# Two-layer sequence kernel: some small loads may be issued on ScalarE's queue, and the norm chains of the attention blocks get an earlier place in the order

## The chip, the cores and the metric

The kernel runs on one core of a Trainium2 chip. The metric is the device time of one execution in microseconds. The core's engines are TensorE (PE: matrix products, transposes; its weight loads are listed apart as PEld), VectorE (DVE), ScalarE (ACT), GpSimd (POOL) and SyncE (SP), which here does nothing but issue DMA transfers. Each engine works through its own instructions in order; semaphores order the engines among each other.

## The reference

The input x is 16 sequences of 256 tokens with 512 channels. Two layers follow each other. The first is a transformer layer with a self-attention, a cross-attention to a second sequence, and an MLP, each with a layer norm ahead of it and a residual sum behind it:

```python
ln_out = layernorm(hidden_states, ln1_s, ln1_b)
qkv = ln_out @ w_qkv + b_qkv
ctx = merge_heads(attention(split_heads(q), split_heads(k), split_heads(v), ltor_mask))
x = hidden_states + (ctx @ w_ao + b_ao)
ln_out = layernorm(x, ln2_s, ln2_b)
...                                   # q from x, k and v from encoder_states
x = x + cross_out
ln_out = layernorm(x, ln3_s, ln3_b)
return x + gelu(ln_out @ w1 + b1) @ w2 + b2
```

Attention has 16 heads of 32 channels and a mask: `scores * mask - 10000 * (1 - mask)`, then a softmax over 256 keys. The second layer mixes each token with the one before it, and carries a state of 16 x 16 for each of 32 heads along the 256 tokens:

```python
a = k_l[..., :, None] * v_l[..., None, :]
out = einsum('bhs,bhst->bht', r_l, faaaa * a + s)
s_new = a + w_l[..., None] * s
...
x = x + y * g @ Wo.T                  # y: out, normalized by head
xc = _ln(x, ln2_w, ln2_b)             # then the channel mix:
x = x + sigmoid(xr2 @ fWr.T) * (square(relu(xk2 @ fWk.T)) @ fWv.T)
```

## The kernel before, in words

**Stages.** The program works in phases, each over the 16 sequences, which it calls batches: A is the self-attention, B the cross-attention, C the MLP, D the token mixing and the projections r, k, v, w and g, I the part of the recurrence inside chunks of 8 tokens, and E the tail. C and D run twice, for batches 0 to 7 and 8 to 15; I is spread in small portions among C, D and E. Between phases the data lies in HBM: x1 after A, x2 after B, x3 after C, then s_r, s_k, s_v, s_w, s_g and what I makes of them (s_y, s_ks, s_rp, s_tot). By the profile A runs from 0 to some 690 us, B to some 1400, the halves of C and D to some 2700 and the tail to the end.

**Products.** Most fp32 products are made of three matmuls of a high and a low part (`mm3`, L495 to L514; the matmuls are L506, L507 and L508).

**Attention, A and B.** `attention` (L774) goes through the 64 groups of four heads. For a group: projection of q and k; scores (L723); on VectorE scale and mask (L730) and row extremes (L736); on ScalarE the exponential (L737); on VectorE a reciprocal of the sums (L740); on POOL the scaling (L743); on TensorE transposes of the probabilities (L756), their copy to SBUF on ScalarE or VectorE (`copy`, L487); and the product with V (L768). A batch ends with the store of x1 or x2.

**The norm chain.** `layer_norm` (L586 to L602) makes, for each half of 128 tokens, statistics (`lnst`, L593, VectorE) and their aggregate (`lnmv`, L594), then adds epsilon (L595, VectorE, the name `lnrs`), raises to the power -1/2 (L596, POOL, the same name), makes the offset (`lnnb`, L597, VectorE) and writes the normalized rows (`xh`), on VectorE or POOL (L600) or ScalarE (L601). TensorE transposes those rows at L613.

**The tail, E.** For each batch `states` (L1391) loads keys (KBc) and spreads them (L1346), and then, for each of two halves of the heads, loads Values with eight transfers of 32 KB into one of two VO tiles (L1410), makes products (L1419), copies the first column, scans (L1426, VectorE), copies (L1427, ScalarE or VectorE) and stores the states with four transfers (`sdr`). `starts` loads them again and spreads them (L1346). `reads` transposes (L1458) and copies (L1469), `heads` multiplies (L1487), and `output`, `residual`, `channels` and `finish` end the batch with products at L1536 and L1578. The functions of different batches are interleaved by the lists `LAG` and `TURNS`.

**What sets the order.** The program first collects all operations with what they read and write. `Sched.run` (L260) then goes through them with planned costs and gives out, step by step, the operation that can start earliest on any engine. An operation may have alternatives on several engines. The key by which one is picked is (L328)

```python
if len(o.alts) > 1:
    s += o.bias.get(e, 0.0)
kx = (max(s - o.urge, f), o.prio, a[1])
```

where `s` is the planned start on that engine, `f` the time at which the engine is free, `o.bias` a handicap for one of several engines, `o.urge` a lead in nanoseconds, and `o.prio` a rank (program order plus an entry of the table `PRIO`). `emit` (L427) looks up rank and urge under the phase and the name of what is written, such as `A.lnst`, and the bias under the phase: POOL has 400 ns in A and B. After an operation its engine's latency from the table `LAT` (L191; SP 950 ns, ACT 128) stands before the operations that wait for it. An operation of the kind `dma` (L479) has the engine SP alone, with 440 ns, and a planned transfer time `o.xfer`. The order so found is written out as each engine's order of instructions, and the chip keeps to it. So one changed number can move instructions in all phases.

Of the kernel before, what the change touches and what calls it, by code (L numbers as in the profile page):

```python
# [16 lines left out]
B, S, C = 16, 256, 512  # L17
# [168 lines left out]
class Sched:  # L186
# [73 lines left out]
    def run(self):  # L260
# [51 lines left out]
        while done < len(ops):  # L312
            best = None
            for e in engs:
                f, c = free[e], None
                for o, a in ready[e]:
                    s = o.t0[e] if o.t0[e] > f else f
                    if e in o.port and port > s:
                        s = port
                    if o.xfer and queues - self.AHEAD > s:  # L320
                        s = queues - self.AHEAD
                    for h in o.banks:
                        for e2, t in used.get(h, {}).items():
                            if e2 != e and t > s:
                                s = t
# [3 lines that stand above are left out]
                    if c is None or kx < c[0]:  # L329
                        c = (kx, o, a)  # L330
                if c is not None and (best is None or c[0] < best[0]):
                    best = c
            assert best is not None, "the streams block each other: " + str({k: [o.i for o in v][:3] for k, v in waits.items() if v})
            _, o, alt = best
            for a in o.alts:
                ready[a[0]].remove((o, a))
            k = can(o)
            if k is not None:
                waits.setdefault(k, []).append(o)
                continue  # L340
            o.eng, o.cost, fn = alt
            o.lat = self.LAT[o.eng]
            t0 = max(o.hold, o.t0[o.eng])
            woken = {}
            for h in sorted((h for h in o.tiles if h.cls is not None and h.t is None), key=lambda h: h.seq):
                if h.cls is not None and h.t is None:
                    t0 = max(t0, mem.ready(h))
                    mem.put(h)
                    woken[h.phase, h.tag, h.cls] = 1
            s = max(t0, free[o.eng])  # L350
            for h in o.banks:
                s = max([s] + [t for e2, t in used.get(h, {}).items() if e2 != o.eng])
            if o.eng in o.port:
                s = max(s, port)
                port = s + o.cost
            if o.xfer:
                s = max(s, queues - self.AHEAD)
            o.start, o.end = s, s + o.cost
            free[o.eng] = o.end
            for h in o.banks:  # L360
                used.setdefault(h, {})[o.eng] = o.end + o.lat
            if o.xfer:
                o.end = queues = max(o.end + self.START, queues) + o.xfer
            if not self.dry:
                fn()
                self.pin()
            for h in o.tiles:
                h.left -= 1
                if h.left == 0 and h.cls is not None:
                    mem.drop(h, o.end + o.lat)  # L370
                    woken[h.phase, h.tag, h.cls] = 1
                    woken[mem.SIZE[h.cls][0]] = 1
            done += 1
            for d in o.outs:
                p = ops[d]
                p.ndep -= 1
                if p.ndep == 0:
                    put(p)
            for k in woken:
                for p in waits.pop(k, []):  # L380
                    put(p)
# [5 lines left out]
def c_act(n, ptr=0, acc=0):  # L387
    return 76.0 + n / 1.2 + 85.0 * ptr + 125.0 * acc
# [14 lines left out]
def c_dma(nbytes, short=False):  # L403

    return nbytes / (146.0 if short else 290.0)


class Kern:
# [18 lines left out]
    def emit(self, eng, cost, fn, r=(), w=(), single=False):  # L427
# [5 lines left out]
        o.bias = BIAS.get(p, {})  # L433
        o.urge = URGE.get(p + "." + (h.split("_")[-1] if h[:1] == "k" and h[1:2].isdigit() else h), 0.0)
        return o
# [40 lines left out]
    def cols(self, ap, n, name):  # L476
        return self.konst([128, n], ap.rearrange("(k p) -> p k", p=128), name)

    def dma(self, h, out, in_, nbytes, r=(), w=None, short=False):  # L479
        o = self.emit("SP", 440.0, lambda: self.nc.sync.dma_start(out=out(), in_=in_()), r=r, w=[h] if w is None else w)  # L480
        o.xfer = c_dma(nbytes, short)
        return o

# [779 lines left out]
class Tail(Rec):  # L1263
# [127 lines left out]
    def states(self, b):  # L1391
# [6 lines left out]
        hk, hv = self.hin["ks"][0], self.hin["v2"][0]  # L1398
# [8 lines left out]
        for hf in range(2):  # L1407
            VO, Sc = self.VO[hf], tile("Sc", [128, 4, 8, 2, 16], "Sc")
            for n in range(8):
                self.dma(None, lambda n=n, VO=VO: VO[16 * n : 16 * n + 16, n, :, :].rearrange("p a v -> p (a v)"), lambda n=n, hf=hf: self.dap("v2", b * S * C + n * 16384 + 512 * hf, [[1024, 16], [1, 512]]), 32768, r=[(hv, b)], w=[(VO, n)])  # L1410
            for pg in (2 * hf, 2 * hf + 1):
                U = tile("p_u", [128, 16, 32], "pu")

                def mm(U=U, pg=pg, VO=VO, hf=hf):
                    for t in range(4):
                        for q in range(4):
                            p = 4 * pg + q
                            n = min(8, 31 - 8 * t)
                            nc.tensor.matmul(U[32 * q : 32 * q + 32, :, 8 * t + 1 : 8 * t + 1 + n].rearrange("p v n -> p n v"), lhsT=KB[t // 2][:, t % 2, p, :], rhs=VO[:, 0:n, 8 * t + p - 8 * hf, :], start=True, stop=True, tile_position=(0, 32 * q))  # L1419

                emit("PE", 900, mm, [VO] + KB, [(U, 1)])
                uc, d0 = (tile(n, [128, 16, 32], n) for n in ("uc", "d0"))
                self.copy(16, lambda U=U: U[:, :, 0], lambda pg=pg: s0[:, 4 * (b % 4) + pg, :], [s0], [(U, 0)])
                emit(("ACT", "POOL"), (c_act(512) + 43, 650), tuple(lambda d0=d0, pg=pg, f=f: f(out=d0(), in_=T[:, b % 4, pg, :].unsqueeze(1).to_broadcast([128, 16, 32])) for f in (nc.scalar.copy, nc.gpsimd.tensor_copy)), [T], [d0])
                flat = lambda t: t().rearrange("p v n -> p (v n)")
                emit("DVE", 1139, lambda uc=uc, d0=d0, U=U: nc.vector.tensor_tensor_scan(out=flat(uc), data0=flat(d0), data1=flat(U), initial=0.0, op0=ALU.mult, op1=ALU.add), [U, d0], [uc])  # L1426
                emit(("ACT", "DVE"), (1066, 700), tuple(lambda uc=uc, Sc=Sc, pg=pg, f=f: f(out=Sc[:, :, :, pg % 2, :].rearrange("p n r v -> p r n v"), in_=uc().rearrange("p v (r n) -> p r n v", n=4)) for f in (nc.scalar.copy, nc.vector.tensor_copy)), [uc], [(Sc, pg % 2)])  # L1427
            for q in range(4):
                self.dma(None, lambda q=q, hf=hf: dr[hf, :, :, q, :].rearrange("n c x -> c n x"), lambda q=q, Sc=Sc: Sc[32 * q : 32 * q + 32].rearrange("p n r g v -> p n (r g v)"), 131072, [Sc], [(dr, (q, hf))])
# [194 lines left out]
    "I": dict(rk=4, P=2, A=1, Y=1),  # L1624
}
PRIO = {"A.pq": -20, "B.pq": -20, "A.pv": 50, "B.x": -400, "B.pv": 50, "A.po": 20, "B.po": -100, "A.x": -50, "A.V": 50, "B.V": 50, "B.qkdr": 20, "B.pc": 20, "A.ks": -20, "A.xh": 20, "B.xh": 400, "B.ks": -20, "B.lnst": -400, "A.rin": -100, "B.rin": -100, "A.E": -50, "A.lnmv": 20, "B.lnmv": 20, "I.P3": -20, "C.xh": -400, "I.r": -100, "E.uc": 100, "D.tt": 20, "I.P2": 20, "C.h": -50, "I.k": 200, "D.s_v": -400, "D.th": -400, "C.ph": -50, "D.x3": -400, "I.v": -20, "I.Y": -100, "D.s_g": -200, "C.g": -200, "E.KBc": -50, "I.s_tot": 200, "C.lnst": 100, "C.po": 400, "D.s1": -400, "E.yT": -400, "E.SBc": -50, "E.xa": 100, "I.s_rp": 400, "E.wst": 20, "I.A": 50, "D.s_k": -20, "D.or": -20, "E.lnst": -20, "E.gr": -200, "C.xT": -200, "D.pt": 20, "D.pd": 50, "E.sq": -100, "C.x": -400, "C.lnmv": -20, "D.ov": 100, "D.x0": -20, "D.ok": 50, "D.lnmv": 100, "D.lnst": -50, "D.xx": -200, "E.gm": 20, "I.s_ks": -20, "D.x": -400, "D.x2": -100, "D.tdr": 100, "C.lnrs": 400, "E.xh": 50, "E.ptr": -100, "D.sx": 20, "E.pr": 200, "E.KB": -50, "D.ow": 100, "E.rp": 400, "D.pz": 50, "D.ptr": 20}
URGE = {n: 200 for n in ('E.gv', 'E.gr', 'E.gt', 'E.lnst', 'E.lnmv', 'E.lnrs', 'E.lnnb')}
AHEAD = [2, 2]
PARTS = [(0, 8), (8, 16)]
AFTER = [7, 4]  # L1630
# [110 lines left out]
```

## Time and profile before

| | |
|---|---|
| median of three runs | 3413.0 us (3410.54 to 3414.68) |
| profiled execution | 3407.0 us |
| span of the profiled execution | 3405.2 us |
| mean granted TensorE clock | 0.975 |
| instructions on TensorE, VectorE, ScalarE, POOL | 27210, 6701, 4750, 1932 |
| bytes moved, mean rate | 334.21 MB, 98 GB/s |
| loads of Values into VO tiles | 256, of 32 KB |

The span runs from the first to the last instruction of the profiled execution. Busy times are given by engine; matmuls are pipelined, and their ends are modelled. A row of the timeline has the start, the length, the engine, the line, the operation with what it writes and reads, and, in square brackets, the idle time of the engine just before it and what ended it. A row of the waits has a total, a number of times and the longest one. SPq is SP's queue of DMA issues. Lines of the form L480 are lines of the kernel before.

### The profile page before, as it was taken

The numbers are of one execution on the slowest core, as the hardware profiler recorded it, in microseconds if no ns is written. First come the engines' busy times: TensorE is split into PE (matmuls) and PEld (weight loads), VectorE is DVE, ScalarE is ACT, GpSimd is POOL, SyncE is SP. The second block draws the span as 40 slices with busy tenths as digits, with TensorE's granted clock in tenths as the row PEclk, the third lists the DMA queues.
The fourth block names the chain that finished last, engine by engine and source line by source line (L and its number), as shares of the span: only waits on it lengthen the run. The fifth ranks groups of instructions, "written<-read, shape, count | busy, mean of one in ns | idle before, by whom it ended". The sixth has DMA issues, their size and how long they took to land. (4 is left out here: it accounts for less than half of the span.)

```text
span 3405.2 us, 73366 instructions
## 1 busy us (share of the span) xinstructions
PE 3196.5 (94%) x27210; PEld 2627.1 (77%) x27210; DVE 2842.5 (83%) x6701; ACT 1878.1 (55%) x4750; POOL 1501.6 (44%) x1932
## 2 busy tenths in 40 slices
PE   7999999999999999899999999999799859999899
PEld 5788777777777777799998888999698745555577
DVE  7888888888888888876788889899889868888786
ACT  6666666666666666633334554434454547565654
POOL 3444444443444444300021127898112766767442
PEclk9999999999999999899999999999899969999999
DMA  3000000121111111310023554434345876765530
GB/s 101 26 26 32 27 29 28 35 79 44 45 45 45 45 45 54 104 33 13 32 75 125 170 180 131 124 117 121 106 152 160 251 230 189 211 195 177 172 120 32
DMA packets 321775, 334.21 MB, mean 98 GB/s; under 512 B 40294, under 2 KB 225166, under 8 KB 321418
## 3 DMA queue, kind: packets, MB, share of 16 engines
q1 hardware_dynamic: 321418, 329.52, 31.1%
q8 instruction: 216, 3.54, 0.4%
q14 instruction: 141, 1.16, 0.1%
HBM read 198.32 MB, written 131.10 MB: 97 GB/s over the span
## 5 line engine op out<-in xcount | busy, mean ns | idle before, releaser
L743 POOL TENSOR_SCALAR slot<-slot,k_rin 128x256 f32<-128x256 f32 x1024 | 489.2, 496 | 619.1 <-DVE k_rin L740 582.7
L492 POOL TENSOR_TENSOR slot<-slot,slot 128x512 f32<-128x512 f32 (+10 forms) x428 | 570.6, 1352 | 339.5 <-ACT slot L571 96.3
L737 ACT ACTIVATE slot<-slot,k_nmx 128x256 f32<-128x256 f32 x1024 | 507.8, 500 | 171.0 <-DVE k_nmx L736 148.5
L506 PE MATMUL bank<-slot,block 128*128 128x256 f32 x2048 | 584.8, 286 | 1.8 <-ACT slot L487 1.3
L507 PE MATMUL bank<-slot,block 128*128 128x256 f32 x2048 | 581.9, 284 | 2.1 <-DVE slot L578 1.4
L508 PE MATMUL bank<-slot,block 128*128 128x256 f32 x2048 | 580.9, 284 | 0.0
L506 PE MATMUL bank<-block,slot 128*128 128x512 f32 x1240 | 502.4, 405 | 4.4 <-DVE slot L577 2.9
L487 ACT ACTIVATE slot<-bank 128x512 f32<-128x512 f32 (+2 forms) x634 | 343.1, 571 | 291.0 <-PE bank L508 148.8
L508 PE MATMUL bank<-block,slot 128*128 128x512 f32 x1240 | 486.6, 392 | 4.5 <-DVE slot L578 2.7
L507 PE MATMUL bank<-block,slot 128*128 128x512 f32 x1240 | 486.4, 392 | 0.0
L506 PEld LDWEIGHTS bank<-slot,block 128*128 128x128 f32 x2048 | 393.5, 192 | 10.6 <-ACT slot L487 3.0
L507 PEld LDWEIGHTS bank<-slot,block 128*128 128x128 f32 x2048 | 393.6, 192 | 9.8 <-DVE slot L623 1.8
L736 DVE CUSTOM_DVE_ANT_0 slot<-slot,slot 128x256 f32<-128x256 f32 x1006 | 398.6, 443 | 0.0
L508 PEld LDWEIGHTS bank<-slot,block 128*128 128x128 f32 x2048 | 393.5, 192 | 0.0
L730 DVE SCALAR_TENSOR_TENSOR slot<-bank,slot 128x512 f32<-128x512 f32 x512 | 330.0, 680 | 53.4 <-PE bank L768 25.1
L756 PE MATMUL bank<-k_c,slot 128*128 128x128 f32 x2048 | 286.3, 280 | 17.6 <-POOL slot L743 13.4
L756 PEld LDWEIGHTS bank<-k_c,slot 128*128 128x128 f32 x2048 | 229.8, 142 | 88.5 <-POOL slot L743 57.5
L506 PE MATMUL bank<-slot,slot 128*128 128x256 f32 (+1 forms) x848 | 276.8, 326 | 13.9 <-ACT slot L577 11.5
L506 PEld LDWEIGHTS bank<-block,slot 128*128 128x128 f32 x1240 | 234.6, 189 | 65.4 <-issue 19.8
L507 PE MATMUL bank<-slot,slot 128*128 128x256 f32 (+1 forms) x848 | 275.5, 325 | 6.6 <-DVE slot L578 6.3
L508 PEld LDWEIGHTS bank<-block,slot 128*128 128x128 f32 x1240 | 233.8, 189 | 59.1 <-DVE slot L578 5.1
L508 PE MATMUL bank<-slot,slot 128*128 128x256 f32 (+1 forms) x848 | 275.0, 324 | 2.4 <-DVE slot L578 2.4
(203 smaller groups left out, 6467.7 us busy)
## 6 DMA issues: line engine op xcount, KB each, us to landing
slot<-in SPq DMA_DIRECT2D x153, 256.0 KB
slot<-x SPq DMA_DIRECT2D x64, 512.0 KB
x<-slot SPq DMA_DIRECT2D x48, 512.0 KB
slot<-in SPq DMA_DIRECT2D x32, 512.0 KB
sdr<-slot SPq DMA_DIRECT2D x128, 128.0 KB
slot<-sdr SPq DMA_DIRECT2D x32, 512.0 KB
s_k<-slot SPq DMA_DIRECT2D x16, 512.0 KB
s_w<-slot SPq DMA_DIRECT2D x16, 512.0 KB
```

Of the source, the lines that this page charges most:

```text
L487: self.emit(("ACT", "DVE"), (c_act(n), c_dve(n)), (lambda: nc.scalar.activation(out=out(), in_=in_(), func=AF.Copy), lambda: nc.vector.ten ...
L492: self.emit(("DVE", "POOL"), (c_dve(n), c_pool(n)), (lambda: nc.vector.tensor_tensor(out=out(), in0=in0(), in1=in1(), op=op), lambda: nc.g ...
L506: nc.tensor.matmul(o, lhsT=lh, rhs=rh, start=first and i == 0, stop=False)
L507: nc.tensor.matmul(o, lhsT=lh, rhs=rl, start=False, stop=False)
L508: nc.tensor.matmul(o, lhsT=ll, rhs=rh, start=False, stop=last and i == k - 1)
L730: emit("DVE", c_dve(512), lambda j=j, T=T: nc.vector.scalar_tensor_tensor(out=T(), in0=ps[j](), scalar=-scale, in1=mask(), op0=ALU.mult, o ...
L736: emit("DVE", c_dve(256) + 80, lambda T=T, j=j, qt=qt: nc.vector.tensor_tensor_reduce(out=T[:, qt, :], in0=T[:, qt, :], in1=negb[:, qt, :] ...
L737: emit("ACT", c_act(256, 1, 1), lambda T=T, Et=Et, j=j, qt=qt: nc.scalar.activation(out=Et[:, qt, :], in_=T[:, qt, :], func=AF.Exp, scale= ...
L743: emit("POOL", 470, lambda jj=jj, qt=qt: nc.gpsimd.tensor_scalar(out=E[jj][:, qt, :], in0=E[jj][:, qt, :], scalar1=rin[:, qt, jj : jj + 1] ...
L756: nc.tensor.transpose(pt[:, k, 128 * qt : 128 * qt + 128], E[j][:, qt, 128 * k : 128 * k + 128], self.ident())
```

## The change

The change has three parts. `dma` gets a parameter `two`: with it an operation has the alternatives SP (440 ns) and ACT (500 ns), ACT with a bias of 300 ns. It is set for Values' loads of the batches 0 to 4 of the tail, which are 80 of the 256; all other transfers stay on SP. The latency that is planned behind a transfer is that of SP, whichever engine issues it. And the table `URGE`, which had seven names of the tail with 200 ns, gets ten more with 200 ns: `lnst`, `lnmv`, `lnrs`, `lnnb` and `xh` of A and of B.

```diff
@@ Sched.run
-            o.lat = self.LAT[o.eng]
+            o.lat = self.LAT["SP" if o.xfer else o.eng]
@@
-    def dma(self, h, out, in_, nbytes, r=(), w=None, short=False):
-        o = self.emit("SP", 440.0, lambda: self.nc.sync.dma_start(out=out(), in_=in_()), r=r, w=[h] if w is None else w)
+    def dma(self, h, out, in_, nbytes, r=(), w=None, short=False, two=False):
+
+        fns = [lambda e=e: e.dma_start(out=out(), in_=in_()) for e in (self.nc.sync, self.nc.scalar)]
+        o = self.emit(("SP", "ACT") if two else "SP", (440.0, 500) if two else 440.0, fns if two else fns[0], r=r, w=[h] if w is None else w)
+        if two:
+            o.bias = {"ACT": 300}
         o.xfer = c_dma(nbytes, short)
         return o
@@ states: the loads of VO
-..., 32768, r=[(hv, b)], w=[(VO, n)])
+..., 32768, r=[(hv, b)], w=[(VO, n)], two=b < 5)
@@
-URGE = {n: 200 for n in ('E.gv', 'E.gr', 'E.gt', 'E.lnst', 'E.lnmv', 'E.lnrs', 'E.lnnb')}
+URGE = {'E.gv': 200, 'E.gr': 200, 'E.gt': 200, 'E.lnst': 200, 'E.lnmv': 200, 'E.lnrs': 200, 'E.lnnb': 200, 'A.lnst': 200, 'A.lnmv': 200, 'A.lnrs': 200, 'A.lnnb': 200, 'B.lnst': 200, 'B.lnmv': 200, 'B.lnrs': 200, 'B.lnnb': 200, 'A.xh': 200, 'B.xh': 200}
```

More of the change, by code (lines that the diff above doesn't have):

```diff
@@ L1409, in states @@
             for n in range(8):
-                self.dma(None, lambda n=n, VO=VO: VO[16 * n : 16 * n + 16, n, :, :].rearrange("p a v -> p (a v)"), lambda n=n, hf=hf: self.dap("v2", b * S * C + n * 16384 + 512 * hf, [[1024, 16], [1, 512]]), 32768, r=[(hv, b)], w=[(VO, n)])
+                self.dma(None, lambda n=n, VO=VO: VO[16 * n : 16 * n + 16, n, :, :].rearrange("p a v -> p (a v)"), lambda n=n, hf=hf: self.dap("v2", b * S * C + n * 16384 + 512 * hf, [[1024, 16], [1, 512]]), 32768, r=[(hv, b)], w=[(VO, n)], two=b < 5)
             for pg in (2 * hf, 2 * hf + 1):
```

## The prediction

> **What bounds the kernel now.** I read the page first, then TensorE's busy time by stretches, its waits, and the timelines of the stretches where it falls short.
>
> ```profile
> PE 3196.5 (94%) x27210; PEld 2627.1 (77%) x27210; DVE 2842.5 (83%) x6701; ACT 1878.1 (55%) x4750; POOL 1501.6 (44%) x1932
> 2680.00:2720.00 40.00, 31.39 (x328) 25.72 (x326) 35.85 (x55) 26.10 (x57) 30.34 (x24) 0.98 0.87 278
> 2720.00:2760.00 40.00, 17.94 (x513) 16.48 (x513) 27.33 (x33) 16.93 (x29) 23.77 (x25) 0.54 0.76 225
> 2760.00:2800.00 40.00, 25.37 (x496) 18.17 (x496) 27.15 (x59) 21.32 (x60) 26.91 (x22) 0.71 0.76 225
> ```
>
> TensorE (the first number after the length of a stretch) is busy for 94% of the span; the rest is small stalls in the attention blocks (0 to 1420 us) and one poor stretch, 2690 to 2840, where the tail starts: from 2720 to 2760 it is busy for 17.94 of 40 us and its granted clock falls to 0.54. These are the two places the change touches.
>
> In self-attention a batch ends with the store of x1. The timeline of SP's queue gives its rhythm:
>
> ```profile
> 175.30 0.37 SPq L480 DMA_DIRECT2D x<-slot  x1
> 215.15 0.37 SPq L480 DMA_DIRECT2D x<-slot  x1
> ...
> 337.99 0.37 SPq L480 DMA_DIRECT2D x<-slot  x1
> 378.55 0.37 SPq L480 DMA_DIRECT2D x<-slot  x1
> 422.67 0.37 SPq L480 DMA_DIRECT2D x<-slot  x1
> 462.98 0.37 SPq L480 DMA_DIRECT2D x<-slot  x1
> 507.10 0.37 SPq L480 DMA_DIRECT2D x<-slot  x1
> 547.49 0.37 SPq L480 DMA_DIRECT2D x<-slot  x1
> ...
> 675.38 0.36 SPq L480 DMA_DIRECT2D x<-slot  x1
> ```
>
> From 175.30 to 378.55 five batches take 40.65 us each. From 378.55 on the intervals alternate, 44.1, 40.3, 44.1, 40.4, and seven average 42.40. The long ones hold one stall: TensorE waits for a copy of transposed probabilities that VectorE does late (waits between 100 and 690 us; then the timelines of TensorE and VectorE).
>
> ```profile
> PE bank L768 <- DVE slot L487: 9.0, 8, 1.9
> 411.46 1.05 PE L768 MATMUL bank<-slot,slot 128*32 128x256 f32 x10 [1.53 <-DVE slot L487]
> 410.64 0.18 DVE L740 RECIPROCAL k_rin<-k_sums 128x4 f32<-128x4 f32 x1 [0.94 <-ACT slot L737]
> 410.73 0.68 DVE L487 COPY slot<-bank 128x512 f32<-128x512 f32 x1
> ```
>
> VectorE stands 0.94 us at a reciprocal that needs ScalarE's exponentials; the copy is behind it in order, and TensorE loses 1.53 us. So the loss is one of order on VectorE, not of work. TensorE never waits for the transposes of the normalized rows (L613): the norm chain is no bound itself.
>
> At the tail's start (TensorE's waits from 2690 to 2960, its first row after the gap, SP's queue, the group of ScalarE's copies):
>
> ```profile
> PE bank L1419 <- DMA block<-s_v: 29.2, 6, 14.2
> PE bank L1487 <- ACT slot L1346: 10.8, 5, 7.4
> 2727.53 3.53 PE L1419 MATMUL bank<-block,slot 128*32 128x128 f32 x64 [14.24 <-DMA block<-s_v]
> 2717.13 2.91 SPq L480 DMA_DIRECT2D block<-s_v  x3
> 2723.62 4.48 SPq L480 DMA_DIRECT2D block<-s_v  x10
> L480 SPq DMA_DIRECT2D block<-s_v x256: 302/418/1981, 2412.0 to 3234.0; - x128
> L1427 ACT COPY slot<-slot 128x512 f32<-128x512 f32 x15 | 16.5, 1103 | 17.1 <-DVE slot L1426 17.1
> ```
>
> TensorE stands 14.24 us, 29.2 in all, for the small loads of Values. Between 2692.9 and 2792.4 SP issues 80 of them, the second half of batch 0 to the first half of batch 5 (the first eight came before 2430), and they hold it 45.7 us, added up row by row: 0.57 each (in the second row shown 4.48/10 = 0.45, in the first 0.97). But the DMA engines themselves are 0.76 to 0.87 busy there.
>
> **The change part by part.** The profiled execution took 3407.0 us (span 3405.2 and 1.8 around it), the median of the three runs is 3413.0. I sum against 3407.0 and add 6.0 at the end.
>
> *Norms first, self-attention.* Of the operations of a norm none is added; what moves is their place in each engine's order and the engine of the last write. By the new order, over both blocks POOL gives up 11 of its writes (0.98 us each by the mean of its row before 1420 us) and VectorE 3 (0.54); ScalarE takes 12 more (the mean of its row is 0.81, so 9.7 us in all); the counts take in a norm or two of the MLP. ScalarE is 55% busy, so 9.7 us over 1400 are beside other work; if that cover were gone they would be the cost. The gain is in the order: in the instruction order of the changed kernel, batches 3 to 13 have the same sequence on every engine, where before no two batches are alike and the last seven alternate. The new sequence on TensorE is that of the former batches of 40.4 to 41.1 us; VectorE's agrees with theirs in 97 of 115 places. I therefore price eleven intervals, 175.30 to 631.05 (the store before the last), at 40.65: 447.2 against 455.8, a gain of 8.6. With twelve it is 12.3. I take 10; bounds 0 (the 18 places differ just where it matters) and 12.3. The other way, a statistic that stands earlier in VectorE's queue can wait for its rows, and all VectorE work behind it with it: L593 waited 16.7 us for loads in both blocks together. If a batch lost half a microsecond more, 16 would give back 8; but from 100 to 690 us it waited only 1.8, so I put nothing.
>
> *Norms first, cross-attention.* Here the batches stay uneven in the new order. Giving each batch the time of the former batch with the nearest order makes 558.7 us of 560.4 for thirteen. Gain 2, bounds -4 and +4, as single batches of the same order differ by up to 2.
>
> *Transitions.* Between the phases matmuls change places. At the tail's start the last projections of the mixing come before the state products that stalled, which fills the gap; but the loads of five weight tiles and three stores now stand on SP ahead of batch 1's first loads, which led them before, and the same kind of bulk stood ahead of the 14.24 us. Before, crossings cost about 17 us (690 to 800) and 13 us (1400 to 1450). No row gives the new cost; half of one such crossing either way is my bound, 8; I take 0, since both kinds of move are seen.
>
> *Values' loads.* The planned latency behind a transfer (the third edit) adds no instruction and is priced with these. 19 of the 80 loads of batches 0 to 4 go to ScalarE in the new order, 3 of them early where TensorE is full; 16 stand in the bad stretch. SP is rid of 16 x 0.57 = 9.1 us. ScalarE takes 16 issues, 9.1 us by SP's row (no row of an issue on ScalarE exists), in 110 us in which it is idle about half. Beside ScalarE's load stands in most cases the copy L1427, which waits for VectorE's scan anyway (17.1 us in 15), so what is queued behind is waiting too: the copies feed the stores of states, and the spreads L1346 feed the reads (10.8 us of waits). The upper end is 9.1, if TensorE's wait of 29.2 shrinks one for one; the lower is a loss of 16 x 1.98 = 31.7, if each issue is held as long as SP's longest and lies on the path. Because SP issues are back to back there and half the DMA time can still bind, I take half of the relief, 4.5. Next late would be the spreads on ScalarE.
>
> The Trainium skill speaks against this part: "DMA: Bandwidth & Descriptors", section "Issuing engines are not separate DMA queues", says that transfers started by different engines share the same sixteen DMA engines and that issuing from several saves only issue time, mostly little beside the transfer. By the row (SP 0.57 us each, back to back) the gain is 4.5 of 9.1, by the rule next to 0. The trace shows DMA at 0.76 busy, so neither is excluded. The same page's "Queues, rings and completion order" says each engine takes turns among queues; by it ScalarE's loads need not stand behind the bulk loads on SP, and the 14.24 us could shrink by more. No run here shows either yet.
>
> Sum: 3407.0 - 10 - 2 - 0 - 4.5 = 3390.5 for a profiled execution, and 3397 as a median.
>
> **The rivals.**
>
> First: the loads' move saves nothing, because the transfers themselves are late. For it: DMA share 0.76 to 0.87 and the loads left on SP (64 of the 80) still end each wait. Against: SP's rows are back to back. 3413 - 12 = 3401.
>
> Second: the even rhythm does not pay. VectorE's new order moves the stall to another copy, or a statistic waits for its rows. For it: 18 of 115 places differ. Against: the short batches ran in nearly this order. Then only cross-attention and the tail are left, between -2 and -6.5: 3407 to 3411, say 3410.
>
> Third, slower: ScalarE is held by its DMA issues. The place is the stretch 2690 to 2800, where ScalarE's spreads and copies stand ahead of TensorE's next products. For it: SP's own issue of this load took up to 1.98 us, the longest of its row. Against: the median is 0.42, and ScalarE is idle for half the time. Price: 31.7 - 9.1 - 12 = +10.6, so 3424. Without relief on SP it decides (over 0.2%) from (12 + 6.8)/16 = 1.2 us for each of 16 exposed holds, with it from 1.75.
>
> **How the numbers follow.** About 0.2% (6.8 us) is what a measurement of this kernel tells from none. My forecast has 0.48, the first rival 0.22, the second 0.16, the third 0.14. Faster by over 0.2% (below 3406.2): the forecast and the first rival nearly whole, and a small part of the second, together 0.70. Same: most of the second, some of the first, 0.16. Slower: 0.14. The range goes down by all gains at their ends (12.3 + 4 + 9.1 + 8 = 33.4: 3379.6, so 3379) and up to 3412, which takes in the second rival and leaves out the third. The likeliest case alone: 3389 to 3404.
>
> **What would show it.** Right: x1 stores 40.4 to 41 us apart from 175 to 630 us, and no 1.5 us stall of TensorE for L487 in these batches; TensorE's wait for Values' loads below 29.2 us by 4 to 9; ScalarE's issues at about 0.5 us each; the waits for L1346 not longer. Wrong: intervals still at 42.4 (second rival); the wait of 29.2 unchanged though SP's rows are fewer (first); ScalarE's issue rows over 1.2 us with longer waits for L1346 and L1427 (third). I would also be wrong if the new crossings cost more than 8 us: then TensorE's busy time from 1400 to 1450 or from 690 to 800 would show it.

## The result: slower by half a percent

The changed kernel takes 3426.7 us (median of five, 3422.4 to 3433.3) against 3413.0 (five, 3409.5 to 3414.7): a ratio of 1.0048, with a 95% interval of 1.0036 to 1.0060, or 12 to 20 us. A gain of 16 us was predicted. Differences given in us below are such a ratio less one, times 3410.

The profiled execution of the changed kernel took 3433.3 us (span 3431.5), 26.3 more than the profiled one of before. That is more than the kernels differ by: the one is the slowest of the five runs, the other lies 2.5 us below the fastest of the five of before. So the two traces tell where time went; how much is told by the ratios of the experiments.

The page after has

```profile
PE 3202.5 (93%) x27210; PEld 2635.1 (77%) x27210; DVE 2862.0 (83%) x6701; ACT 1875.2 (55%) x4754; POOL 1503.7 (44%) x1928
```

**Where the time went.** The stores of x1, x2, x3, s_k and of the results on SP's queue are marks that both traces have. After less before, in the profiled executions: the 15th x1 of self-attention -0.7, the 16th -2.1, last x2 +3.3, last x3 of the first half -2.2 and of the second +9.8, last s_k ahead of the tail -2.9. Then, in SP's timeline, the changed kernel first:

```profile
2687.13 0.36 SPq L481 DMA_DIRECT2D s_k<-slot  x1
...
2873.60 0.39 SPq L481 DMA_DIRECT2D out_dram<-slot  x1
...
3362.42 65.64 SPq L481 DMA_DIRECT2D out_dram<-slot  x4
```

and before:

```profile
2690.05 0.36 SPq L480 DMA_DIRECT2D s_k<-slot  x1
...
2857.27 0.39 SPq L480 DMA_DIRECT2D out_dram<-slot  x1
...
3336.17 65.64 SPq L480 DMA_DIRECT2D out_dram<-slot  x4
```

Up to the tail nothing is lost. That the changed kernel is 3 us ahead there is not more than traces of one order differ by: at the same store the seven runs below that keep the order of before up to the tail (e4, e5, e6, e7, e10, e13, e14) stand 1.6 to 6.0 us ahead of the trace of before. Then 19 us go between the last s_k and the first result (186.5 us against 167.2; against the traces of e7, e8, e9 and e14, in which this stretch takes 169 to 170 us, some 17), 10 more behind it. The whole loss is in the tail.

**Self-attention.** The new rhythm of the x1 stores is even, as forecast, but for some batches, and the stall of 1.5 us is gone:

```profile
217.33 0.37 SPq L481 DMA_DIRECT2D x<-slot  x1
258.17 0.37 SPq L481 DMA_DIRECT2D x<-slot  x1
299.02 0.37 SPq L481 DMA_DIRECT2D x<-slot  x1
341.06 0.37 SPq L481 DMA_DIRECT2D x<-slot  x1
381.90 0.37 SPq L481 DMA_DIRECT2D x<-slot  x1
```

The intervals are 40.85, and 42.0 in the third shown. What the long one holds is in the timelines of VectorE, POOL and TensorE, and in VectorE's waits from 176 to 630 us:

```profile
DVE k_lnst L597 <- DMA slot<-in: 17.4, 11, 2.8
305.47 0.69 DVE L597 BATCH_NORM_STATS2 k_lnst<-slot 128x6 f32<-128x512 f32 x1 [2.81 <-DMA slot<-in]
309.39 1.84 POOL L747 TENSOR_SCALAR slot<-slot,k_rin 128x256 f32<-128x256 f32 x4 [5.29 <-DVE k_rin L744]
309.92 1.00 PE L760 MATMUL bank<-k_c,slot 128*128 128x128 f32 x4 [0.41 <-POOL slot L747]
```

The statistics now stand ahead of the row extremes in VectorE's queue, and wait in every batch for the rows to land, 17.4 us in 11 waits; before, 1.8 us. Most of these waits hide (1.3 us each); when one lasts 2.8 us, the reciprocal, POOL's scaling and TensorE's transposes behind it come late. TensorE's row shows 0.41 us of that, of the 1.2 us that this batch is longer; that the stand makes the long interval is read from these rows, and no run shows it by itself.

The order, and no scatter, makes the difference: the eleven intervals from the third store on last 451.2 to 452.3 us in the four traces with the changed order (the changed kernel, e3, e8, e15) and 455.7 to 455.9 in the ten with the old one.

**The tail's start.** The same windows as before, TensorE's waits from 2690 to 2960 us, and rows of SP's queue, TensorE, ScalarE and its queue:

```profile
2680.00:2720.00 40.00, 28.18 (x267) 24.15 (x265) 34.35 (x55) 25.57 (x55) 30.26 (x21) 0.92 0.84 276
2720.00:2760.00 40.00, 16.53 (x516) 15.17 (x516) 25.79 (x32) 17.99 (x36) 20.04 (x23) 0.63 0.71 202
2760.00:2800.00 40.00, 19.70 (x467) 16.94 (x468) 20.50 (x42) 17.50 (x46) 20.57 (x17) 0.59 0.73 213
```

```profile
PE bank L1423 <- DMA block<-s_v: 19.8, 4, 11.8
PE bank L1423 <- DMA sdr<-slot: 14.2, 1, 14.2
PE bank L1491 <- DVE slot L1350: 10.0, 3, 8.7
PE bank L1423 <- DVE slot L1350: 10.0, 1, 10.0
2739.51 0.90 SPq L481 DMA_DIRECT2D block<-s_v  x2
2742.59 3.54 PE L1423 MATMUL bank<-block,slot 128*32 128x128 f32 x64 [14.22 <-DMA sdr<-slot]
2746.18 0.81 ACTq L481 DMA_DIRECT2D block<-s_v  x2
2747.09 1.07 ACT L1431 COPY slot<-slot 128x512 f32<-128x512 f32 x1 [8.69 <-DMA block<-s_v]
L481 ACTq DMA_DIRECT2D block<-s_v x19: 308/347/433, 2418.9 to 2774.8; - x19
```

By the names in these rows TensorE's wait for Values' loads fell from 29.2 to 19.8 us. But the 14.2 us put down to the stores `sdr` are a wait for Values' loads too. In the changed kernel's list of instructions the products at 2742.59 wait for the loads of their VO tile and for no store. The last two of these loads were issued from 2739.51 on, behind four stores of states, and by the trace's semaphore events the last one landed at 2742.35; a store landed just behind it and gave the wait its name. So this wait rose, from 29.2 to 34.0 us (in e3 below, the same order with all loads on SP, it is 39.0). The waits for the spreads, 10.8 us before, rose to 21.0 (L1350 here, with 1.0 for spreads on POOL).

ScalarE's issues are short, 0.31 to 0.43 us. But the copy at 2747.09 comes 8.69 us after ScalarE's work before it, and for 7.8 of them ScalarE stood in front of the two issues at 2746.18. By the list these loads wait for the products that read the same VO tile, those of 2742.59, and they went out 0.05 us after the end of these (2742.59 + 3.54 = 2746.13). TensorE is busy 10.3 us less than before over these three windows.

### The profile page after: what moved, and what is told of

Same layout as the page of the kernel before. It is cut to its first block, busy times and chain, and to the rows that moved or that the text cites. A ratio compares the mean times of both kernels' runs of the same rounds, so it can differ in the third digit from the quotient of the medians.

```text
span 3431.5 us, 73382 instructions
## 1 busy us (share of the span) xinstructions
PE 3202.5 (93%) x27210; PEld 2635.1 (77%) x27210; DVE 2862.0 (83%) x6701; ACT 1875.2 (55%) x4754; POOL 1503.7 (44%) x1928
## 3 DMA queue, kind: packets, MB, share of 16 engines
q8 instruction: 216, 3.54, 0.4%
## 4 chain that ended last, share of the span: by engine, by line
PE 63%; DVE 9%; issue 4%; DMA 3%; ACT 2%; POOL 1%; SPq 1%; DVEq 0%; ACTq 0%; POOLq 0%
PE bank L510 14%; PE bank L512 14%; PE bank L511 14%; PE bank L1540 6%; PE bank L760 3%; PE bank L1582 2%; PE bank L617 2%; PE bank L772 2%; PE bank L1423 1%; PE bank L727 1%; ACT slot L741 1%; PE bank L1491 1%; DVE slot L740 1%; SPq L481 1%; PE bank L1076 1%
## 5 line engine op out<-in xcount | busy, mean ns | idle before, releaser
L496 POOL TENSOR_TENSOR slot<-slot,slot 128x512 f32<-128x512 f32 (+10 forms) x443 | 595.0, 1361 | 370.0 <-ACT slot L575 116.0
L491 ACT ACTIVATE slot<-bank 128x512 f32<-128x512 f32 (+3 forms) x631 | 341.2, 570 | 257.5 <-PE bank L512 138.6
```

The source lines that it names most:

```text
L491: self.emit(("ACT", "DVE"), (c_act(n), c_dve(n)), (lambda: nc.scalar.activation(out=out(), in_=in_(), func=AF.Copy), lambda: nc.vector.ten ...
L496: self.emit(("DVE", "POOL"), (c_dve(n), c_pool(n)), (lambda: nc.vector.tensor_tensor(out=out(), in0=in0(), in1=in1(), op=op), lambda: nc.g ...
```

## The experiments

The list in which the scheduler gives out its 14980 operations can be written down and spliced: at many places the lists of the two kernels have done the same set of operations, only in another order. A kernel can so have one kernel's order in one stretch and the other's elsewhere.

### One part of the change alone: e1_norms_only and e2_loads_only

```diff
 e1: -URGE = {n: 200 for n in ('E.gv', ...)}
     +URGE = {'E.gv': 200, ..., 'A.lnst': 200, ..., 'B.xh': 200}
 e2: the other edits, URGE as before
```

> The kernel before with the ten new names in the table of leads alone; all loads stay on SP. Theory 1 (the tail is slower because the operations stand in another order there, which the norms' part alone already changes): about 3420 to 3427, with the tail (from the last projections to the end) 15 to 25 us longer than before and self-attention within 2 us. Theory 2 (the tail is slower because ScalarE's queue is held by the loads): 3400 to 3413, tail as before.

> The changed kernel with the old table of leads: only Values' loads may go to ScalarE. Theory 1 (order): anything from -5 to +15 us against 3413, as the order of the tail is a third one; self-attention as before (store intervals of 44.1 and 40.4). Theory 2 (ScalarE held): 3425 to 3435, with waits of ScalarE of 5 us or more in front of its load issues.

Measured: e1 1.0008 (0.9997 to 1.0019), e2 0.9995 (0.9983 to 1.0008). Neither half of the change is measurably slower or faster; e1 (3412.4 us) misses what theory 1 expected of it, e2 (3406.9) what theory 2 did. So the loss is no property of one half: the order that comes out of both together is a third one.

### The loads back on SP, in the new order; the loads on ScalarE, in the old: e3_plan_sp and e4_before_act

```diff
 e3: -for e in (self.nc.sync, self.nc.scalar)]
     +for e in (self.nc.sync, self.nc.sync)]
 e4 (kernel before): -self.nc.sync.dma_start(...)
     +(self.nc.scalar if two else self.nc.sync).dma_start(...)   # two=0 < b < 5 and n % 4 == 3
```

> The changed kernel with its order kept on every engine, but the 19 loads that stood on ScalarE are issued by SP at the same place in the overall order. Theory 1 (order): as the changed kernel, 3422 to 3430, or slower by the 9 us of issues that SP gets back. Theory 2 (ScalarE held): the loss in the tail is gone, 3400 to 3412.

> The kernel before with its order kept, but 16 loads (every fourth of the batches 1 to 4) are issued by ScalarE at the same place in the overall order. Theory 1 (order): 3405 to 3416, as the queue hardly matters. Theory 2 (ScalarE held): 3423 or more, with waits of ScalarE of 5 us or more in front of its load issues.

Measured: e3 1.0036 (1.0022 to 1.0051), e4 1.0013 (1.0002 to 1.0024). The order alone costs about 12 of the 16 us, the queue about 4, in either order. The queue's part is small beside the noise: the intervals of the changed kernel and of e3 overlap, and e4's just leaves out 1. The traces point the same way: from the last s_k to the first result the changed kernel takes 186.5 us and e3 180.8; e4 takes 171.7 and the kernel before 167.2. So theory 1 has the larger part, theory 2 a smaller one. How the queue costs is in SP's waits from 2690 to 2900 us; of e4, then of the changed kernel:

```profile
SPq L480 <- DMA block<-s_v: 23.1, 9, 6.1
SPq L481 <- DMA block<-s_v: 9.4, 8, 2.3
```

In the kernel before and in e3 there is no such wait. The order of SP's instructions in e4, with the semaphores each waits for, says why. Each transfer that SP or ScalarE issues takes one of eight semaphores, in strict turn, and most wait first for the one that they take (lines between 652 and 656 left out):

```
649 L480 DMACopy block2_30109<-s_v2_65 16x512 [waits DMAHW2_49]
650 L480 DMACopy block2_30109<-s_v2_65 16x512 [waits DMAHW4_49]
651 L480 DMACopy block2_30109<-s_v2_65 16x512 [waits DMAHW5_49]
652 L480 DMACopy block2_30109<-s_v2_65 16x512 [waits DMAHW6_49]
656 L480 DMACopy block2_30109<-s_v2_65 16x512 [waits DMAHW3_49]
```

DMAHW3, passed over from 649 to 650, went to ScalarE's load; SP's transfer eight turns later, 656, waits for it. By this list a transfer that waits so may not start before the one eight places ahead in the common order has landed, so SP waits for a load that ScalarE has not come to yet, and ScalarE's loads wait for SP's. The trace of e4 shows the same: SP's longest wait of this kind ends with its issue at 2720.05, which takes the semaphore of a load that ScalarE issued at 2715.26 and that landed at 2719.98. In this program two queues bring no more than eight transfers under way, and tie the two engines to each other.

### The loads on a queue with semaphores of its own: e10_pool

```diff
 e4: -(self.nc.scalar if two else self.nc.sync).dma_start(...)
 e10: +(self.nc.gpsimd if two else self.nc.sync).dma_start(...)
```

> As e4_before_act (order before, 16 loads moved), but they are issued by GpSimd, whose transfers have eight semaphores of their own in the program; SP's and ScalarE's share one set of eight. If SP was held because its transfers take turns on the same eight semaphores with loads that ScalarE had not yet issued: SP's waits for Values' loads, 23.1 us in 9 in e4, fall below 3 us, and the time is 3405 to 3412 unless GpSimd's issues take long. If SP was held by the transfers as such (the DMA engines are full): the waits stay above 10 us and the time is 3412 to 3418.

Measured: 0.9969 (0.9956 to 0.9982), or 3399.5 us, 11 us faster than before (6 to 15) and below what either case expected, where the same 16 loads on ScalarE were 4 us slower. SP's wait for Values' loads is gone altogether, although GpSimd's issue is the longer one. Of the loads, and TensorE's waits from 2690 to 2960 us:

```profile
L480 POOL DMA_DIRECT2D block<-s_v x16: 484/546/748, 2697.6 to 2774.7; - x16
PE bank L1419 <- DMA block<-s_v: 18.2, 3, 12.0
```

This agrees with the shared semaphores as the queue's cost. It is not proof that they alone make the gain: SP is rid of sixteen issues here, 9.1 us by the prediction's rows, which lies within the interval, and GpSimd's loads also run on another kind of queue (`software_dynamic` in the profile, where SP's and ScalarE's are `hardware_dynamic`). Neither was tried by itself.

### Which stretch: e5_start_act, e6_start_sp, e7_rest, e8_early

```diff
 e5: [0:11960] before, [11960:12509] after, [12509:] before; 16 loads on ScalarE
 e6: the same, all loads on SP
 e7: [0:12509] before, [12509:] after; all loads on SP
 e8: [0:11960] after, [11960:] before; all loads on SP
```

> The order of all operations is written down as a list instead of planned: the list of the kernel before, and in one stretch, the start of the tail (the 549 operations that take the states of batches 0 to 4), the list of the changed kernel, 16 loads on ScalarE among them. If the start of the tail makes the loss (theory A): 3420 to 3430. If the loss comes from the rest of the tail (theory B) or is made by norms-first before the tail (theory C): 3408 to 3416.

> The same stretch of the changed kernel's list inside the list before, but the 16 loads issued by SP. Theory A with the queue as the cause: 3408 to 3416, as before; theory A with the order as the cause: 3418 to 3426. Theories B and C: 3408 to 3416.

> The list before up to the end of that stretch, and from there to the end of the kernel the list of the changed kernel; all loads on SP. Theory B: 3420 to 3430, and TensorE's wait for L1356 (7.2 us in both) stays. Theories A and C: 3408 to 3416.

> The list of the changed kernel up to the start of the tail (attention, MLP and mixing, with the norm chains first), and the list before from there on; all loads on SP. Theory C: 3420 or more. Theories A and B: 3407 to 3413, since by the stores before the tail the changed kernel is 2 us ahead there; self-attention in even batches of 40.85 us but for those where VectorE waits over 2 us for its rows.

| stretch of the new order | ratio | interval | us |
|---|---|---|---|
| e8: all ahead of the tail | 0.9996 | 0.998 to 1.0011 | -1.4 |
| e6: start of the tail, loads on SP | 1.0007 | 0.9997 to 1.0017 | +2.4 |
| e5: start of the tail, loads on ScalarE | 1.0016 | 1.0006 to 1.0026 | +5.5 |
| e7: rest of the tail | 1.0032 | 1.0020 to 1.0045 | +10.9 |

e8, e5 and e7 make up the changed kernel, and -1.4 + 5.5 + 10.9 = 15.0 stands against its 16.4; each of these has some 4 us of noise either way, and the next two runs show that stretches need not add up. By these runs two thirds of the loss lie in the order of the rest of the tail, where the change has no edit: the five batches of loads are over, and the norms with a new lead are long done. Theory B was the main one, A a smaller part, C fell.

### The rest of the tail, split: e13_rest_first and e14_rest_second

```diff
 e13: the list before, with [12509:12933] of the changed kernel
 e14: the list before, with [12933:14030] of the changed kernel
```

> Half of e7: the list before, with the list of the changed kernel only for the 424 operations that follow the start of the tail (some 2800 to 2900 us); all loads on SP. If the loss of 10.7 us lies in one place of the tail's order, either this kernel or e14_rest_second has 8 to 12 us of it and the other none; this one by the first stores of results in e7 (9 us late at 2938): 3416 to 3421.

> The other half of e7: the list of the changed kernel only for the next 1097 operations of the tail (some 2900 to 3200 us); all loads on SP. If the loss is in one place and that is the first half: 3407 to 3412. If it is spread over the tail as idle time and lower granted clock: about half of it in each, 3413 to 3416 in both.

Measured: e13 1.0042 (1.0028 to 1.0057), e14 1.0018 (1.0007 to 1.0029). The first stretch alone costs as much as the whole rest in e7, the second about 6 us; their sum, 20.4, is above e7's 10.9, though behind 14030 the two lists agree and these two stretches are all of e7. So stretches do not add up here; a cost of the splice at its seam would be one reason, and no run shows it. In e13's SP timeline the first result is stored at 2856.48 and the fourth at 2994.64, 138.2 us; in the kernel before at 2857.27 and 2984.17, 126.9 us. In e14 these four results take 139.5 us and in e7 139.9, so either stretch alone makes the delay and both together make it once. Windows of e13 there:

```profile
2860.00:2880.00 20.00, 14.81 (x362) 13.25 (x349) 13.05 (x30) 10.12 (x25) 11.26 (x11) 0.83 0.44 118
2900.00:2920.00 20.00, 14.49 (x319) 10.06 (x318) 15.24 (x30) 6.66 (x21) 15.31 (x17) 0.76 0.75 222
```

and of the kernel before:

```profile
2860.00:2880.00 20.00, 17.31 (x381) 13.26 (x384) 14.50 (x34) 10.16 (x27) 15.52 (x15) 1.00 0.69 225
2900.00:2920.00 20.00, 17.15 (x369) 13.07 (x371) 18.47 (x33) 11.91 (x33) 17.66 (x20) 1.00 0.77 217
```

TensorE is idle 2.5 us more in each of the two, and the granted clock (third number from the end) is lower in both. Over 2840 to 3000, the clock missing in slices of 20 us, times 20, makes 12.2 us in e13 and 5.2 before. No wait in TensorE's list explains the idle time: most of it is put down to nothing that the profile shows. What in this order costs it stays open.

### Is the stand at the statistics what took self-attention's gain? e11_no_stats_lead

```diff
-'A.lnst': 200, ... 'B.lnst': 200,      # the other new names stay; order before from the MLP on
```

> The table of the changed kernel without a lead for the statistics (lnst) of self- and cross-attention; that order to the first half of the MLP, from there the list before, all loads on SP. If VectorE's stand at the statistics (17.4 us in 11 between 176 and 630 us) is what took the gain of the even batches: that wait falls below 6 us, the intervals of the x1 stores are 40.4 to 40.7 us without one of 42, and the time is 3402 to 3407. If the even batches simply last 40.85 us by TensorE's work: intervals unchanged, 3408 to 3413.

Measured: 1.0014 (1.0003 to 1.0025). Inconclusive: VectorE's wait did not fall (16.5 us in 11); the intervals are 40.85 and at times 41.2 to 41.4. So the wait could not be taken away in this way, and what it costs stays open. 40.85 is what the new order gives without a long wait; in the changed kernel TensorE is busy for 40.3 us of such an interval.

### A gain that is given back, and the best version: e9_middle, e12_middle_pool

```diff
 e9: the list before, with [10061:11471] of the changed kernel (second MLP half to second mixing half)
 e12: e9, and the 16 loads of e10 on GpSimd
```

> The list of the kernel before, with the changed kernel's list only for the stretch from the middle of the second half of the MLP to the middle of the second half of the mixing (1411 operations). By the stores of the runs so far the changed order gains 6 to 11 us there against the order before, whatever comes ahead of it and behind it. If gains and losses of stretches add up: 3400 to 3406, ratio 0.997 to 0.9985. If a gain there is given back in the tail (which then starts the same work 6 to 11 us earlier, at a time when its loads are late): 3408 to 3414.

> The middle stretch of e9 and the 16 loads on GpSimd of e10 together, all else in the order before. If the two gains add: 3409 - 3 - 11 = 3395. If the earlier start of the tail in e9 was given back because the loads were late, and the loads are now sooner: down to 3388. If GpSimd's loads only bring what the earlier start would bring: 3399 to 3403.

Measured: e9 0.9993 (0.9985 to 1.0002), e12 0.9957 (0.9942 to 0.9972). In e9's profile the stretch itself gains 10 us (x3 stores 3.2 us ahead of the kernel before, s_k stores 12.5 to 13.5), and the tail gives most of it back: 11.2 us ahead at the first result, 5.4 at the fourth, 1.8 at the last. In e12, with GpSimd's loads, it is 19.5, 14.6 and 14.0 ahead. e12 takes 3393.9 us as a median of four, 15 us less than the kernel before, and beats both kernels.

### The changed kernel with its loads on GpSimd: e15_after_pool

```diff
-for e in (self.nc.sync, self.nc.scalar)]
+for e in (self.nc.sync, self.nc.gpsimd)]
```

> The changed kernel, with its 19 loads issued by GpSimd at the place where ScalarE issued them. If the shared set of eight semaphores and ScalarE's own standing were the queue's cost, it falls below e3_plan_sp (3421): 3408 to 3416, with no wait of SP for Values' loads. If GpSimd's gain in e10 belongs to the order before alone: 3420 to 3427.

Measured: 1.0017 (1.0007 to 1.0027), against 1.0048 on ScalarE and 1.0036 on SP; SP's wait for Values' loads is 1.3 us. The queue's cost turned into a gain in this order too, of some 6 us against e3, about as much as the two intervals can tell apart; the kernel is still 6 us slower than the one before.

## Why the prediction was wrong

**Self-attention, -10.** The mechanism was right: an even rhythm, no 1.5 us stall. The size failed at two steps. I took 40.65 us for the new interval from five old ones that I read as alike; they run from 39.4 to 42.4, and 40.65 is only their mean. The new order takes 40.85, with some of 42.0: 451.8 us for the eleven intervals from the third store on, where I put 447.2 and before had 455.8. And I priced VectorE's stand at the statistics at nothing, because it waited only 1.8 us before; it became 17.4, and the two longest of these waits, 2.8 and 2.7, lie in the two intervals of 42.0. That they make these intervals is likely and not shown. The irregular batches at both ends took 3 of the 4 us gained, so the phase gave 0.7 at the 15th store.

**Cross-attention, -2.** It went the other way: from 3.3 us ahead at the first x2 store to 3.3 behind at the last, past my bound of +4. The fifteen intervals between these stores last 650.8 to 652.0 us in the four traces with the changed order, 642.8 to 645.1 in the ten with the old one. TensorE's wait for POOL's scaling, 11.4 us before between 760 and 1420 us, is 14.6, which is half of it; the rest stays open. Giving each new batch the time of the old one with the nearest order was not good enough.

**Transitions, 0 with 8 either way.** Not shown wrong as a sum: e8 has -1.4 us (-7 to 4) for everything ahead of the tail, and the new start of the tail with its loads on SP +2.4 (e6, -1 to 6). It hides a loss between MLP and mixing (2.2 us ahead at the last x3 store of the first half, 6.9 behind at the s_k store that follows it) and a gain of 6 to 10 us at the second one, so that it came out near 0 is in part luck.

**Values' loads, -4.5.** The move cost some 3 us (e5 less e6, within the noise) to 4 us (e4, just clear of it) instead. The failing step is "SP is rid of 16 x 0.57 us", with nothing put down for what SP gets in return: SP waited 9.4 us in 8 for loads that ScalarE issued, as much as it was to be rid of, because the transfers of both engines take turns at eight semaphores. TensorE's wait for these loads, which was to shrink by 4 to 9 us, is 34.0 instead of 29.2. The 0.57 was also too large: the merged rows that I added up hold the gaps between their issues, and the 80 issues alone make 38.4 us, 0.48 each. The instruction order with its semaphores would have told of the turns beforehand. Of the third rival, the place and the sign were right and the mechanism half: ScalarE was held and the waits for the spreads were longer, but it was held once for 7.8 us by a load that waited for its VO tile to be read, not 16 times by the issuing, which took 0.31 to 0.43 us each.

The Trainium skill's rule that was weighed, "DMA: Bandwidth & Descriptors", section "Issuing engines are not separate DMA queues", gave next to 0 for the loads; that was nearer than my 4.5. The measured move to ScalarE is worse than its rule, under which a second engine saves the time of issuing and nothing more: it cost time, by the tie between the queues. The move to GpSimd gained 11 us (6 to 15), which the time of issuing, 9.1 us by my rows, can account for.

**What was not in the sum at all.** The tail behind its start, 10.9 us in e7, the largest single part of the loss. I compared the order of the tail only up to the first batches and let the rest stand at zero without a bound. A scheduler that plans the whole program moves all that comes after an edit, and a term for that belonged in the sum, as the tail has waits to gain or lose (before, TensorE is idle for 42 of the 496 us from 2840 to 3336). With that term bounded by what the transitions were (8 either way), the range would have reached 3420, still short of the 3426.7 measured. What in the new order of the tail costs the time stays open.

## What to carry to other kernels

Before a transfer is moved to another engine's queue, look in the order of instructions at which semaphore it takes: if both queues share one set in turn, the move adds no transfers under way, and makes each engine wait for the other's progress. Here the same sixteen loads cost 4 us on the queue that shares the set and gained 11 on the one with a set of its own. Where one scheduler orders the whole program, every edit is also a draw of a new order for all later phases: compare the order to the very end, give the untouched phases a bound in the sum, and splice old and new order to tell the edit's own effect from the draw's.

## What the runs showed of the hardware

A DMA issue on ScalarE took 0.31 to 0.43 us in the changed kernel, one on SP 0.30 to 2.86 us for the same load, one on GpSimd 0.48 to 0.75 us, with a median of 4.4 us from issue to landing (e10). Sixteen loads of 32 KB moved to GpSimd shortened the kernel by 11 us, with the DMA engines' mean share at 0.79 and 0.87 in the two windows of 40 us between 2720 and 2800 us (0.76 in both before): at 0.76 they were not full.
